# Layer norm in the loaded tile, and a residual that a DMA adds in DRAM

## The chip, the cores and the metric

The kernel runs on one NeuronCore of a Trainium2 chip. The metric is the device time of one execution in microseconds (us), the median of several runs; lower is better. The engines are called PE (matmul), DVE (vector), ACT (scalar), POOL (GpSimd) and SP (which here only issues DMAs). Each works through its own queue strictly in order.

## The reference, cut to what matters

The input is an image of shape (2, 256, 64, 64), seen as two sequences of 4096 positions with 256 channels. Three stages follow: a state-space scan over a group-normed input (layer 0), a bidirectional scan block, and a mixture of eight small feed-forward experts. The change lies in the middle block:

```python
def _core(x, ln_gamma, ln_beta, fp, bp):
    mu = x.mean(-1, keepdims=True)
    var = x.var(-1, keepdims=True)
    xn = (x - mu) / jnp.sqrt(var + 1e-05) * ln_gamma + ln_beta
    y_fwd = _mamba(xn, *fp)
    y_bwd = jnp.flip(_mamba(jnp.flip(xn, 1), *bp), 1)
    return y_fwd + y_bwd + x
```

Here the block's input is itself already a normalised tensor. The kernel therefore takes two roots from one variance: `r1`, which normalises the incoming tensor into the block's `x`, and a second factor that gives `xn` from it in one step. The block's output is the sum of both scans, of `x`, and of the tensor before that normalisation; the running sum is kept in DRAM as `t_dram`.

## The kernel before

**Jobs, chunks, slots.** There are six scan jobs: for each of the two batches a layer-0 job (256 inner channels), a forward job and a backward job (512 inner channels each; the code calls the backward one `flip`). A job runs over 8 chunks of 512 positions. A chunk of 256 inner channels is 16 slots long, one of 512 is 32. In each slot DVE does one scan instruction (L774, 128x1024), so the starts of the 1280 scans tell which slot runs at which time. Numbering the chunks 0 to 47, the forward chunks are 8 to 15 and 32 to 39, the backward ones 16 to 23 and 40 to 47.

**The work of a slot.** POOL forms the scan's input (`bq`, L738) and multiplies some results by C (L799); ACT forms the decays (`da`, L748) in PSUM; DVE scans (L774) and multiplies the other results by C (L783); PE sums over the states (L807).

**The order.** A table (`sl.put(slot, queue, fn)`) places everything else by hand: the next chunk's preparation, the previous chunk's output projection, weight loads. What is put is emitted in slot order, and each engine keeps that order. A planner (`experts`) fills PE and ACT room that is left, by counts of planned work (`sl.count`), with the experts' matmuls of finished columns; what does not fit there is done after the last scan, in a second stage bound to PE.

**The layer norm of a forward chunk** (`norm`, L350 to L445) runs about 45 slots ahead of its chunk. SP loads the columns from `t_dram` into tile `x` (`load_x`, L371); PE takes the mean (L390); DVE writes `cen` = `x` - mean (L396); ACT squares it into tile `nx` (L400); PE takes the variance (L405); ACT takes the two roots; DVE forms the normalised residual in `nx` (L415) and the doubly normalised tensor in `cen` (L416); POOL adds the residual, `x += nx` (L419); ACT then writes gamma and beta applied to `cen` into `nx` (L423), which overwrites what POOL has just read; SP stores `nx` to `n2_dram` for the backward job (L429) and `x` back to `t_dram` (L430). Tile `x` has one buffer and is also used by layer 0; `nx` has two; `cen` has one.

**The output of a chunk** (`finish`, L822 to L857): SP loads the running sum into `xr` (one buffer, L830), PE projects and adds (L837, L839) at slots 16 and 18 of the next chunk (7 and 8 for a 256-channel job), ACT copies into `xr` (L854), SP stores to `t_dram` (L855). The load stands 10 slots before the end of the chunk, and not before slot 21 when the chunk before was a 512-channel one.

**Features** (`features`, L859 to L898), after each backward chunk but the last: mean of `xr`, `fcen` = `xr` - mean by DVE into tile `cen` (L872), squares on ACT, variance, divide by DVE (L887), store to `nf_dram` (L892) for the experts.

**The softplus part of a chunk's preparation** (L582 to L598) holds a tile of three shared buffers named `th` until SP has stored it (`dtd<-sp`, L598).

Of the kernel before, what the change touches and what calls it, by code (L numbers as in the profile page):

```python
# [42 lines left out]
F32 = mybir.dt.float32  # L43
AF = mybir.ActivationFunctionType
ALU = mybir.AluOpType
AX = mybir.AxisListType

P = 128
NB, C, L = 2, 256, 4096
KC = C // P  # L50
T = 512
NCH = L // T
# [19 lines left out]
SLOTS = {  # L72
    2: dict(xs=(-23, -22), conv=(-20,), dbc=-16, dt=(-14, -13), z=(-10, -9), out=(7, 8)),
    4: dict(
        xs=(-31, -30, -24, -23), conv=(-26, -21), dbc=-17, dt=(-15, -13, -11, -9), z=(-6, -5, -3, -2),
        out=(16, 18),
    ),
}
AHEAD = 3
# [55 lines left out]
def hybrid_kernel(ctx: ExitStack, tc: tile.TileContext, a: dict, out: bass.AP):  # L135
    nc = tc.nc
# [14 lines left out]
    mean_w = mean_col.to_broadcast([P, P])  # L151
# [17 lines left out]
    t_dram = [drp.tile([P, KC, L], F32, name=f"t_dram{b}") for b in range(NB)]  # L169
# [10 lines left out]
    def rsqrt(dst, src, eps, scale=1.0):  # L180
        nc.scalar.activation(dst, src, AF.Ln, bias=eps, scale=scale)
        nc.scalar.activation(dst, dst, AF.Exp, scale=-0.5)

    def over_channels(t):
        return t.rearrange("p (o t) -> p o t", o=1).to_broadcast([P, KC, T])
# [6 lines left out]
    with ExitStack() as st:  # L192
        wp = st.enter_context(tc.tile_pool(name="wp", bufs=1))
        wk = st.enter_context(tc.tile_pool(name="wk", bufs=1))
# [19 lines left out]
        sl = Slots()  # L214
# [130 lines left out]
        steps = [(job, c) for job in jobs for c in range(NCH)]  # L345
        starts = [sum(8 * job.nj for job, _ in steps[:i]) for i in range(len(steps) + 1)]
# [3 lines left out]
        def norm(i):  # L350

            (job, c), ck, tag, s0 = steps[i], cks[i], tags[i], starts[i]
            s = job.cols(c)
            b = job.batch
            if job is jobs[AHEAD]:
                return

            def alloc():
                ck["nx"] = wk.tile([P, KC, T], F32, tag="nx", name=f"nx_{tag}", bufs=2)

            if job.flip:
                def load():
                    alloc()
                    nc.sync.dma_start(ck["nx"], n2_dram[b][:, NCH - 1 - c, :, :])
                sl.put(s0 - 44, "sp", load)
                return

            def load_x():
                ck["x"] = wk.tile([P, KC, T], F32, tag="x", name=f"x_{tag}")
                src = t_dram[b] if job.layer else a["x"][b].rearrange("(k p) l -> p k l", p=P)  # L370
                nc.sync.dma_start(ck["x"], src[:, :, s])  # L371

            if job.layer == 0:
                def scale():
                    alloc()
                    for k in range(KC):
                        nc.scalar.activation(
                            ck["nx"][:, k, :], ck["x"][:, k, :], AF.Identity,
                            bias=job.gb[:, k : k + 1], scale=job.gs[:, k : k + 1],
                        )  # L380
                sl.put(s0 - 32, "sp", load_x)
                sl.put(s0 - 25, "act", scale)
                return

            def mean():
                ck["ps"] = psp.tile([P, T], F32, tag="ps", name=f"mean_{tag}")
                for k in range(KC):
                    nc.tensor.matmul(  # L390
                        ck["ps"], mean_w, ck["x"][:, k, :], start=(k == 0), stop=(k == KC - 1)
                    )

            def centre():
                ck["cen"] = wk.tile([P, KC, T], F32, tag="cen", name=f"cen_{tag}")
                nc.vector.tensor_tensor(ck["cen"], ck["x"], over_channels(ck["ps"]), ALU.subtract)  # L396

            def square():
                alloc()
                nc.scalar.activation(ck["nx"], ck["cen"], AF.Square)  # L400

            def variance():
                ck["var"] = psp.tile([P, T], F32, tag="ps", name=f"var_{tag}")
                for k in range(KC):
                    nc.tensor.matmul(  # L405
                        ck["var"], mean_w, ck["nx"][:, k, :], start=(k == 0), stop=(k == KC - 1)
                    )

            def roots():
                ck["r1"] = psp.tile([P, T], F32, tag="ps", name=f"r1_{tag}")  # L410
                rsqrt(ck["r1"], ck["var"], eps5)
                rsqrt(ck["var"], ck["var"], eps10, scale=1.0 + 1e-5)

            def divide():
                nc.vector.tensor_tensor(ck["nx"], ck["cen"], over_channels(ck["r1"]), ALU.mult)  # L415
                nc.vector.tensor_tensor(ck["cen"], ck["cen"], over_channels(ck["var"]), ALU.mult)  # L416

            def add():
                nc.gpsimd.tensor_tensor(ck["x"], ck["x"], ck["nx"], ALU.add)  # L419

            def affine():
                for k in range(KC):
                    nc.scalar.activation(  # L423
                        ck["nx"][:, k, :], ck["cen"][:, k, :], AF.Identity,
                        bias=lngb[:, 1, k : k + 1], scale=lngb[:, 0, k : k + 1],
                    )

            def store():
                nc.sync.dma_start(n2_dram[b][:, c, :, :], ck["nx"])  # L429
                nc.sync.dma_start(t_dram[b][:, :, s], ck["x"])  # L430

            late = 1 if NCH < i < 2 * NCH else 0
            for d, queue, fn in (
                (-48, "sp", load_x), (-44, "pe", mean), (-43, "dve", centre), (-42, "act", square),
                (late - 41, "pe", variance), (late - 40, "act", roots), (late - 39, "dve", divide), (late - 39, "pool", add),
                (-35 if c else -38, "act", affine), (-34, "sp", store),
            ):

                sl.put(s0 + d + (6 if c == 0 else 0), queue, fn)
            s0 += 6 if c == 0 else 0  # L440
            sl.count(s0 - 44, 2, 0, (1,))
            sl.count(s0 - 43, 0, 1)
            sl.count(s0 - 41, 2, 4, (2,))
            sl.count(s0 - 40, 0, 0, (1,))
            sl.count(s0 - (36 if c else 39), 0, 2.3)  # L445
# [376 lines left out]
        def finish(i):  # L822
            (job, c), ck, tag = steps[i], cks[i], tags[i]
            s, b = job.cols(c), job.batch
            v = {}

            def load():
                v["x"] = wk.tile([P, KC, T], F32, tag="xr", name=f"xr_{tag}")
                src = t_dram[b] if job.layer else a["x"][b].rearrange("(k p) l -> p k l", p=P)
                nc.sync.dma_start(v["x"], src[:, :, s])  # L830

            def over_time(m):
                return v["x"][:, m, ::-1] if job.flip else v["x"][:, m, :]

            def project(m):
                v[m] = psp.tile([P, T], F32, tag="ps", name=f"o_{tag}_{m}")
                nc.tensor.matmul(v[m], ident, over_time(m), start=True, stop=False)  # L837
                for j in range(job.nj):
                    nc.tensor.matmul(  # L839
                        v[m], job.w["out"][:, j, m * P : (m + 1) * P], ck["sz", j],  # L840
                        start=False, stop=(j == job.nj - 1),
                    )

            s0 = starts[i + 1]

            before = steps[i - 1][0].nj if i else 0
            sl.put(max(s0 - (10 if job.nj == 4 else 5), starts[i] + (21 if before == 4 else 0)), "sp", load)

            slots = SLOTS[job.nj]["out"] if i + 1 < len(steps) else (3, 4)
            for slot in slots:  # L850
                sl.count(s0 + slot, 1 + job.nj, 1, (1,))
            for m, slot in enumerate(slots):
                sl.put(s0 + slot, "pe", lambda m=m: project(m))
                sl.put(s0 + slot + 1, "act", lambda m=m: nc.scalar.copy(over_time(m), v[m]))  # L854
            sl.put(s0 + slot + 2, "sp", lambda: nc.sync.dma_start(t_dram[b][:, :, s], v["x"]))  # L855
            if job.flip and i + 1 < len(steps):
                features(b, NCH - 1 - c, v, s0 + slot + 2)  # L857

        def features(b, c, v, s0):  # L859
# [8 lines left out]
                    )  # L868

            def centre():  # L870
                v["cen"] = wk.tile([P, KC, T], F32, tag="cen", name=f"fcen_{b}{c}")
                nc.vector.tensor_tensor(v["cen"], v["x"], over_channels(v["ps"]), ALU.subtract)  # L872

            def square():
# [217 lines left out]
        for g in range(nq):  # L1092
            i, jp, n = quads[g]
# [47 lines left out]
    with ExitStack() as st:  # L1141
# [5 lines left out]
        n, x, y, acc, wts, wb, lt, w_dram = {}, {}, {}, {}, {}, {}, {}, {}  # L1147
        q = T // P
# [417 lines left out]
```

## Time and profile before

| | |
|---|---|
| median of 3 runs | 5031.76 us (5031.76 to 5034.15) |
| the profiled execution | 5034.19 us, of which the span from first to last instruction is 5032.4 us |
| busy in the span | POOL 4361.3 us, DVE 4569.8, PE 4249.7, ACT 3614.0 |
| scans (chunks 0 to 47) | 62 to 4476 us; the rest is the experts' second stage |
| forward chunks | 530.5 to 1428.2 us and 2729.0 to 3607.9 us |
| backward chunks | 1428.2 to 2299.3 us and 3607.9 to 4476.4 us |

Busy time adds the durations of instructions. A DVE or POOL instruction starts a little before the one ahead of it has ended, so sums of busy time can exceed the stretch they are taken over; how long an engine stood idle is read from its waits.

### The profile page before, as it was taken

How to read it: one execution, taken by the hardware profiler on the slowest of the kernel's cores; microseconds unless marked ns; L12 is line 12 of the kernel's file. 1: busy time of each engine (PE TensorE's matmuls, PEld its weight loads, DVE VectorE, ACT ScalarE, POOL GpSimd, SP SyncE). 2: the span in 40 equal slices, each digit the busy share in tenths (PEclk: the TensorE clock that was granted, in tenths of full speed). 3: DMA queues.
4: the chain of work that ended last, by engine and by line, in shares of the span. 5: the costliest groups of instructions: out<-in, count | busy, mean ns of one | idle time of the engine just before them, and what ended most of it. 6: DMA issues, size and time to landing. Idle time of an engine off the chain costs nothing. (4 is left out here: it accounts for less than half of the span.)

```text
span 5032.4 us, 47312 instructions
## 1 busy us (share of the span) xinstructions
PE 4249.7 (84%) x14912; PEld 1477.5 (29%) x14912; DVE 4569.8 (91%) x3097; ACT 3614.0 (72%) x7303; POOL 4361.3 (87%) x1426
## 2 busy tenths in 40 slices
PE   5777778788777899989999998989868899889998
PEld 1222222222222233333333332323212333234443
DVE  6998999999999999999989999999999999955654
ACT  5777777777777787887787788878767878752222
POOL 5998999999999999999999999999999999950000
PEclk8778889899887999999999999999989999999999
DMA  5445444444454555447675555554434554446643
GB/s 190 154 171 183 158 167 154 154 152 156 153 176 138 180 173 172 160 169 246 243 240 207 174 173 185 169 186 171 158 131 155 181 195 168 170 151 217 208 155 117
DMA packets 334319, 875.26 MB, mean 174 GB/s; under 512 B 36250, under 2 KB 111796, under 8 KB 292084
## 3 DMA queue, kind: packets, MB, share of 16 engines
q1 hardware_dynamic: 329140, 842.73, 48.6%
q0 software_dynamic: 4928, 29.51, 1.7%
q8 instruction: 118, 1.93, 0.2%
q14 instruction: 133, 1.09, 0.1%
HBM read 673.27 MB, written 198.84 MB: 173 GB/s over the span
## 5 line engine op out<-in xcount | busy, mean ns | idle before, releaser
L738 POOL TENSOR_TENSOR bq<-rxdt,bc 128x2048 f32<-128x2048 f32 x640 | 2892.5, 4542 | 17.3 <-DMA rxdt<-xdtd 9.8
L748 ACT ACTIVATE da<-rdt,w_a 128x512 f32<-128x512 f32 x2560 | 1757.3, 686 | 109.9 <-DVE bq L774 63.4
L774 DVE TENSOR_TENSOR_SCAN da<-da,h_state,bq 128x1024 f32<-128x1024 f32 x664 | 1559.0, 2348 | 55.0 <-ACT da L748 44.9
L799 POOL TENSOR_TENSOR bq<-bq,bc 128x2048 f32<-128x2048 f32 (+1 forms) x280 | 1180.0, 4214 | 22.5
L774 DVE TENSOR_TENSOR_SCAN bq<-da,h_state,bq 128x1024 f32<-128x1024 f32 x456 | 1059.9, 2340 | 23.4 <-ACT da L748 23.4
L807 PE MATMUL y<-bq,stack 128*32 128x512 f32 x5120 | 747.8, 670 | 267.5 <-POOL bq L799 244.0
L783 DVE TENSOR_TENSOR bq<-da,bc 128x1024 f32<-128x1024 f32 x760 | 927.1, 1220 | 15.7
L988 PE MATMUL e<-eh,ew 128*128 128x512 f32 x1376 | 670.2, 621 | 64.8 <-DVE sp L587 12.6
L793 ACT COPY h_state<-da 128x2 f32<-128x2 f32 x759 | 119.1, 157 | 619.6 <-DVE bq L783 617.8
L759 ACT ACTIVATE bq<-h_state,bq,a 128x1 f32<-128x1 f32 x1120 | 429.9, 384 | 2.8 <-POOL bq L738 2.2
L988 PEld LDWEIGHTS e<-eh,ew 128*128 128x128 f32 x1376 | 250.4, 194 | 475.6 <-issue 234.9
L451 PE MATMUL z<-nx,w_in 128*128 128x512 f32 x640 | 329.4, 644 | 62.3 <-DVE nx L415 21.0
L807 PEld LDWEIGHTS y<-bq,stack 128*32 128x32 f32 x5120 | 140.9, 116 | 812.4 <-POOL bq L799 350.1
L524 PE MATMUL conv<-xs,w_conv 64*64 64x512 f32 x2560 | 330.3, 602 | 22.5 <-ACT xs L508 20.3
L1317 ACT ACTIVATE h<-hp,of,sc 128x512 f32<-128x512 f32 x168 | 130.5, 777 | 302.8 <-PE hp L1313 288.7
L988 PE MATMUL e<-en,ew 128*128 128x512 f32 x688 | 323.3, 603 | 24.8 <-DVE fcen L887 17.2
L451 PE MATMUL xs<-nx,w_in 128*128 128x512 f32 x640 | 317.6, 625 | 21.3 <-DVE xc L537 8.5
L839 PE MATMUL o<-sz,w_out 128*128 128x512 f32 x640 | 296.0, 602 | 0.0
L1001 ACT ACTIVATE eh<-e,of,sc 128x512 f32<-128x512 f32 x344 | 259.1, 767 | 44.3 <-PE e L988 44.1
L591 POOL TENSOR_TENSOR xdt<-sp,xc 128x512 f32<-128x512 f32 x160 | 203.3, 1275 | 46.1 <-DVE sp L587 46.1
L774 DVE TENSOR_TENSOR_SCAN da<-da,bq 128x1024 f32<-128x1024 f32 x96 | 219.5, 2286 | 4.4 <-ACT da L748 2.4
L814 PE MATMUL y<-xc,w_d 128*128 128x512 f32 x320 | 186.6, 667 | 20.0 <-DVE sz L820 19.8
(144 smaller groups left out, 4722.0 us busy)
## 6 DMA issues: line engine op xcount, KB each, us to landing
rxdt<-xdtd SPq DMA_DIRECT2D x160, 1024.0 KB, 6.8
rdt<-dtd SPq DMA_DIRECT2D x160, 1024.0 KB, 6.5
bc<-bcd SPq DMA_DIRECT2D x384, 256.0 KB, 3.2
ew<-in_W SPq DMA_DIRECT2D x172, 256.0 KB, 5.0
u<-u SPq DMA_DIRECT2D x86, 512.0 KB, 5.8
u<-eu SPq DMA_DIRECT2D x82, 512.0 KB, 4.3
dtd<-sp SPq DMA_DIRECT2D x160, 256.0 KB, 3.5
xdtd<-xdt SPq DMA_DIRECT2D x160, 256.0 KB, 3.4
```

The costliest lines, as they stand in the source:

```text
L451: nc.tensor.matmul(ps, job.matrices["in", half][:, k, j * P : (j + 1) * P], rhs, start=(k == 0), stop=(k == KC - 1),)
L524: nc.tensor.matmul(v[r][64 * col : 64 * col + 64, :], job.matrices["conv"][rows, 2 * jp + j, k, :], ck["xs", jp][rows, j, k : k + T] if k ...
L738: nc.gpsimd.tensor_tensor(bq[g], ck["rxdt", j], over_groups(ck["bc", 0, sg]), ALU.mult)
L748: nc.scalar.activation(da[g, h][:, k, :], cks[i]["rdt", j][:, q, :], AF.Exp, scale=steps[i][0].w["a"][:, j, q * SG + sg : q * SG + sg + 1],)
L759: nc.scalar.activation(bq[g][:, q, 0:1], job.h[:, j, sg, q : q + 1], AF.Identity, scale=cks[i]["a0", j][:, h, sg : sg + 1], bias=bq[g][:, ...
L774: nc.vector.tensor_tensor_scan(b if on_pool(g, h) else d, d, b, job.h[:, j, sg, 2 * h : 2 * h + 1] if c else 0.0, ALU.mult, ALU.add,)
L783: nc.vector.tensor_tensor(bq[g][:, two, :], d, cks[i]["bc", 1, sg].rearrange("p (o t) -> p o t", o=1).to_broadcast([P, 2, T]), ALU.mult,)
L799: nc.gpsimd.tensor_tensor(b, b, cks[i]["bc", 1, sg].rearrange("p (o t) -> p o t", o=1).to_broadcast([P, groups, T]), ALU.mult,)
L807: nc.tensor.matmul(y[i, j][q * CG : (q + 1) * CG, :], stack, bq[g][:, q, :], start=False, stop=(sg == SG - 1),)
L839: nc.tensor.matmul(v[m], job.w["out"][:, j, m * P : (m + 1) * P], ck["sz", j], start=False, stop=(j == job.nj - 1),)
L988: nc.tensor.matmul(ps, ew[l][:, k, m * P : (m + 1) * P], key[x][:, k, :], start=(k == 0), stop=(k == KC - 1),)
L1001: nc.scalar.activation(key[dst][:, m, :], key["ps", l, m], AF.Relu, bias=of[:, l, e, m : m + 1], scale=sc[:, l, e, m : m + 1],)
```

## The change

It changes where the layer norm of a forward chunk is worked, who adds its residual, and where the features are worked.

- `load_x` of a forward chunk takes one of the two `nx` buffers at the load, at slot -48 instead of at the squares at -42, and the columns are loaded into it. Mean, centre, second division and affine all work in that tile.
- The squares go to a tile `q` of the tag `x`, which later takes the normalised residual.
- POOL's add is replaced by a DMA that POOL issues, which adds `q` to `t_dram` in DRAM. The store of `x` by SP is gone.
- The features' centre works in `xr` itself, so `xr` is held until the store to `nf_dram`.
- The load of `xr` in a backward chunk moves from 10 slots before its end to 2 slots before it.
- The last backward chunk of the first batch (chunk 23) projects at slots 7 and 8 of the next chunk instead of 16 and 18, and its features follow from there.

```diff
 def load_x():
-    ck["x"] = wk.tile([P, KC, T], F32, tag="x", name=f"x_{tag}")
+    if job.layer:
+        alloc()
+        ck["x"] = ck["nx"]
+    else:
+        ck["x"] = wk.tile([P, KC, T], F32, tag="x", name=f"x_{tag}")
...
 def centre():
-    ck["cen"] = wk.tile([P, KC, T], F32, tag="cen", name=f"cen_{tag}")
-    nc.vector.tensor_tensor(ck["cen"], ck["x"], over_channels(ck["ps"]), ALU.subtract)
+    nc.vector.tensor_tensor(ck["x"], ck["x"], over_channels(ck["ps"]), ALU.subtract)

 def square():
-    alloc()
-    nc.scalar.activation(ck["nx"], ck["cen"], AF.Square)
+    ck["q"] = wk.tile([P, KC, T], F32, tag="x", name=f"q_{tag}")
+    nc.scalar.activation(ck["q"], ck["x"], AF.Square)
...
 def divide():
-    nc.vector.tensor_tensor(ck["nx"], ck["cen"], over_channels(ck["r1"]), ALU.mult)
-    nc.vector.tensor_tensor(ck["cen"], ck["cen"], over_channels(ck["var"]), ALU.mult)
+    nc.vector.tensor_tensor(ck["q"], ck["x"], over_channels(ck["r1"]), ALU.mult)
+    nc.vector.tensor_tensor(ck["x"], ck["x"], over_channels(ck["var"]), ALU.mult)

 def add():
-    nc.gpsimd.tensor_tensor(ck["x"], ck["x"], ck["nx"], ALU.add)
+    nc.gpsimd.dma_start(t_dram[b][:, :, s], ck["q"], accum_op=ALU.add)
...
 def store():
     nc.sync.dma_start(n2_dram[b][:, c, :, :], ck["nx"])
-    nc.sync.dma_start(t_dram[b][:, :, s], ck["x"])
...
-    sl.put(max(s0 - (10 if job.nj == 4 else 5), starts[i] + (21 if before == 4 else 0)), "sp", load)
-    slots = SLOTS[job.nj]["out"] if i + 1 < len(steps) else (3, 4)
+    sl.put(max(s0 - (2 if job.flip else 10 if job.nj == 4 else 5), starts[i] + (21 if before == 4 else 0)), "sp", load)
+    slots = SLOTS[2 if i == AHEAD * NCH - 1 else job.nj]["out"] if i + 1 < len(steps) else (3, 4)
...
 # features
-    v["cen"] = wk.tile([P, KC, T], F32, tag="cen", name=f"fcen_{b}{c}")
+    v["cen"] = v["x"]
     nc.vector.tensor_tensor(v["cen"], v["x"], over_channels(v["ps"]), ALU.subtract)
```

## The prediction

> **What bounds the kernel now.** I first cut the span by stages. The slices of the page show POOL and DVE at 9 in almost every slice up to about 4476 us, and the starts of the scans give the chunks. The windows view over one forward chunk of each batch and one backward chunk then reads (columns: stretch, its length, then busy us and instructions of PE, PEld, DVE, ACT and POOL, the granted clock, DMA):
>
> ```profile
> 862.90:975.60 112.70, 89.17 (x358) 28.26 (x357) 111.18 (x78) 88.17 (x184) 112.14 (x39) 0.89 0.46 160
> 3057.60:3167.50 109.90, 99.22 (x365) 34.59 (x364) 108.06 (x71) 90.45 (x185) 109.34 (x36) 0.97 0.52 174
> 4042.10:4150.90 108.80, 99.62 (x365) 34.13 (x364) 106.67 (x70) 88.04 (x182) 107.66 (x35) 0.97 0.53 179
> ```
>
> POOL is busy for 112.1 of 112.7 us, 109.3 of 109.9 and 107.7 of 108.8. The 2.8 us between the two forward chunks are about the two extra POOL products (1.27 us each) that batch 0 carries for the work done ahead for batch 1. So POOL sets the pace of a forward chunk. DVE is close behind. The waits view of DVE over the first of these chunks has one wait worth the name (us, times, longest):
>
> ```profile
> DVE da L774 <- ACT da L748: 0.9, 1, 0.9
> ```
>
> The same view of POOL there has no line at all. Over the six forward chunks in which norms run (8 to 13, 530.5 to 1313.5 us with chunk 14) POOL waits 0.6 us. Who is held by the add itself is in the view of L419:
>
> ```profile
> L419 POOL TENSOR_TENSOR x<-x,nx x16: 2337/2349/2380, 402.7 to 3371.8; 128x1024 f32<-128x1024 f32 x16
> ...
> who waited for it (us, times):
>   ACT nx L423: 5.3, 6
>   DVE da L774: 0.4, 1
> ```
>
> ACT's affine waits for the add, because it overwrites what the add reads. In chunk 11 ACT stands 0.88 us before L423 at 966.39 us, the next decay is late, and that is DVE's 0.9 us.
>
> Backward chunks have another picture. SP's waits, DVE's waits over 3607.9 to 4368.5 us, what ACT's L582 waits for, and a piece of SP's timeline:
>
> ```profile
> SPq L830 <- DVE fcen L872: 35.9, 15, 4.8
> ```
> ```profile
> DVE sp L587 <- ACT h_state L793: 6.3, 6, 1.5
> ```
> ```profile
>   DMA dtd<-sp: 24.4, 10
> ```
> ```profile
> 4110.66 0.57 SPq L598 DMA_DIRECT2D xdtd<-xdt  x1
> 4113.65 0.55 SPq L830 DMA_DIRECT2D xr<-t_dram  x1
> 4114.29 0.55 SPq L598 DMA_DIRECT2D dtd<-sp  x1
> ```
>
> SP stops at the load of `xr`, whose buffer is freed by the features' centre; the store of the softplus tile queues behind it, together with 512 KB of load. The chain that ended last runs through exactly this store (4.81 us from 4114.29 us). ACT then lacks a `th` buffer, and DVE stands 1.0 to 1.6 us per chunk at L587.
>
> **What the Trainium skill says.** "GPSIMD Engine Reference", section 3.1, gives 4497 ns for a two-input add of 2048 floats on POOL; here L738 takes 4542 and the half-sized L419 2349, so the page agrees. "DMA: Bandwidth & Descriptors", section "SWDGE vs HWDGE vs iDMA", says that an accumulating DMA has to be issued by GpSimd, whose cores write its descriptors; so POOL still pays something for each. "SBUF — State Buffer", section "Who interferes with whom", says that a DVE instruction with at most one SBUF input does not contend with GpSimd. The scan and L783 read one operand from PSUM; DVE's L783 takes 1220 ns beside a POOL that never rests, which fits.
>
> **The change part by part.**
>
> *A. POOL in forward chunks.* Removed: 16 adds of 2.35 us, 37.6 us. Added: 16 DMA issues. The trace has no accumulating issue into DRAM. The nearest rows are the 13 issues of L1202, some of which accumulate, and the one plain issue on the strided `t_dram`:
>
> ```profile
> L1202 POOL DMA_DIRECT2D nm<-nf_dram x13: 528/556/897, 4538.1 to 4832.6; - x13
> ```
> ```profile
> L1169 POOL DMA_DIRECT2D n<-t_dram x1: 717/717/717, 4831.9 to 4831.9; - x1
> ```
>
> The plain ones take 0.53, the accumulating 0.89, the strided layout adds 0.19; and the one issue that follows an arithmetic instruction directly (4466.62 us) took 0.73 where its like took 0.53. I take 0.89 + 0.19 = 1.1 us; the bounds are 0.7 and, with the last 0.2 doubled, 1.5. That is 17.6 us, so POOL has 20 us less to do (14 to 26), 1.25 us per norm.
> How much of it comes out depends on DVE. Without its waits DVE needs about 111.7 of the 112.7 us in batch 0 (it waits 0.9 + 0.2), and in batch 1 about 108.3 of 109.9 (the like chunk 2947 to 3058 has 1.1 + 0.4 + 0.2). Its main wait there is the one behind the add, which goes too. So I take 1.0 us per chunk in batch 0 and 1.1 in batch 1, six chunks each: 12.6 us. The other four norms (of chunks 8, 9, 32, 33) run in layer-0 chunks where DVE waits mostly for ACT and PE (1.7 at the mean and 2.0 at the roots for chunk 8): 0.6 each, 2.4 us. Bounds for A: 6 (DVE gives only half) and 20 (POOL alone).
>
> *B. SP in forward chunks.* One 512 KB store (0.54 us of issue) less per norm. SP is not on the path there: nothing gained. Loading into `nx` six slots earlier waits for the buffer of two chunks before, whose last reader is at slot -66 against -48: nothing. At the first norm, layer 0 and the norm share the two buffers; the last layer-0 scale then waits for the gate matmul of the chunk before, over at 365.9 us, and ACT gets there at 369.1. The load itself no longer waits for that scale (SP stood until 370.67 us), worth 0 to 3 us in a chunk of 61 us; I take 1.
>
> *C. Backward chunks.* The load of `xr` leaves slot 22, so SP's 35.9 us there go, and the store of the softplus tile lands about 2 us earlier. DVE's waits at L587, 6.3 us in each batch, would vanish. But POOL is nearly full here too: its own waits over chunks 16 to 22 and 40 to 46 are 3.8 and 2.5 us, 6.3 in all, and no more can come out. I take 4 (0 to 6.3). At its new place, slot 30, the load needs the `nf_dram` store landed: issued near slot 28, 3.9 us to landing, so SP may stop for up to 2 us, with stores of that moment behind it that nobody waits for within two slots. The projection is 18 slots away. For the very last chunk the load falls at about 4466 us and PE needs it at 4483.99: covered; without that cover it would cost its 5 us.
>
> *D. Centre in place.* DVE now has to wait until the store of `xr` (L855) has been read out. Landing takes 3.1 us in the median; the centre starts 4.4 to 4.6 us after the issue in most chunks, and the least slack seen is 0.4 us. Behind it on DVE stand the scans. I take 1 us in all, bounds 0 and 6.
>
> *E. Chunk 23's projection at 7 and 8.* Its last gate is at slot 2, so PE has what it needs. Its work moves 9 to 10 slots earlier in the planner's counts. Worked through by the planner's rule, the experts placed stay 86, with shifts of a few slots between 640 and 805 only; the second stage keeps its 42. I take 0 (-3 to 3).
>
> Sum: -12.6 - 2.4 - 1 - 4 + 1 = -19. I keep 17, since DVE, ACT and POOL are all within 2% of full and small delays of one show in the others. The profiled execution took 5034.2, 2.4 above the median; taken from the median, 5031.8 - 17 = **5015 us**.
>
> **Rivals.**
> *1. POOL alone binds.* Then A gives all 20, C its 6 and B 3: about 5031.8 - 29 = 5003. For it: POOL has no wait. Against: DVE has 1.1 us of slack per chunk.
> *2. DVE is the wall already.* The 0.9 us behind the add turns up at another ACT wait, A gives 4, C 1, D takes 1: about 5028. For it: L587's wait lies where POOL is full.
> *3. Slower: descriptor writing is held up by DVE.* "SBUF — State Buffer" has a case of an issue of 620 ns that took 3100 beside a DVE copy. If the 1.1 us became 1.1 + 2.5 = 3.6, POOL would have 16 x 1.25 = 20 us more; less C that is 5048. It decides from 2.35 us per issue on. Against: no DVE copy stands in those chunks, and the issue at 4466.62 us, with DVE scanning, took 0.73.
> That the sum doesn't stay off POOL is rival 3; that the DMA orders after some other transfer of `t_dram` is no better founded, since the store L430 waits for no such transfer now.
>
> **How the numbers follow.** A measurement can tell 0.2%, 10 us. Main case 0.53, rival 1 0.16, rival 2 0.17, rival 3 0.14. Faster by more than 10 us: nearly all of the first two, 0.68; within: rival 2 and a remnant, 0.18; slower 0.14. The range goes from 4999, under rival 1, to 5036, over rival 2 with D at its bound; it leaves out rival 3 and the far end of rival 1.
>
> **What would show it.** Right: L419 a DMA issue of about 1.1 us; forward chunks of 111.7 and 108.9 us instead of 112.7 and 110; no wait of ACT's L423 on POOL; in backward chunks no wait of DVE at L587 and SP's wait on the centre gone; waits of DVE at the centre under 0.3 us each. Wrong: an issue over 2 us, POOL waits before it, or forward chunks unchanged with DVE free of waits (rival 2).

## The result, and the profile after

| | before | after |
|---|---|---|
| median | 5031.76 us (20 runs) | 5024.28 us (20 runs) |
| ratio, 95% interval | | 0.9984 (0.9978 to 0.9990) |
| span of the profiled execution | 5032.4 us | 5019.1 us |
| POOL busy | 4361.3 us | 4342.0 us |

The change saves 7.5 us; the interval of the ratio allows 5 to 11. The forecast was 5015, a gain of 17. The sign was right and the time lies in the range, but the gain is under half the forecast, less than the 10 us that the prediction called tellable, and nearer to rival 2 (5028). The two profiled executions differ by 13.3 us, of which 5.8 lie in the second stage; runs of other kernels below spread from 549.6 to 557.2 us in that stage, so nothing is read from it.

I cut both traces at the starts of the scans, as in the prediction. Each number of the next table is the difference of two such starts, in us (chunk 47 ends with its last scan), from one trace of each kernel; the last columns are experiments told below.

| chunks | before | after | forward alone | backward alone | load alone | chunk 23 as before | xs earlier |
|---|---|---|---|---|---|---|---|
| 9-13, forward, batch 0 | 563.8 | 567.3 | 567.2 | 564.1 | 563.8 | 567.2 | 563.4 |
| 16-22, backward, batch 0 | 761.4 | 755.2 | 760.5 | 756.1 | 755.3 | 755.4 | 755.4 |
| 23, the turn | 109.7 | 112.1 | 110.2 | 112.6 | 112.1 | 112.0 | 110.8 |
| 24-31, layer 0, batch 1 | 429.7 | 430.9 | 427.6 | 434.4 | 430.0 | 429.8 | 430.4 |
| 32-39, forward, batch 1 | 878.9 | 872.6 | 872.1 | 877.5 | 879.0 | 872.3 | 872.0 |
| 40-46, backward, batch 1 | 760.6 | 755.7 | 760.3 | 754.4 | 755.3 | 755.1 | 755.4 |
| 47, the last | 108.0 | 110.4 | 109.3 | 110.3 | 109.4 | 109.5 | 111.3 |

The gain is in the backward chunks and in batch 1's forward chunks. Batch 0's forward chunks, from which I expected most, became slower.

**POOL got what was promised.** The windows view of the kernel after, over a forward chunk of each batch, with the columns of the prediction:

```profile
863.60:976.80 113.20, 90.18 (x358) 27.53 (x357) 111.29 (x78) 88.19 (x184) 110.89 (x38) 0.91 0.47 159
3052.60:3162.40 109.80, 98.27 (x366) 34.11 (x364) 108.13 (x71) 90.53 (x186) 108.15 (x36) 0.97 0.55 176
```

The fifth busy column, POOL, fell from 112.14 to 110.89 in the first row, the 1.25 us per norm of the prediction. Yet the chunk takes 113.2 us instead of 112.7. The issue in the view of L422:

```profile
L422 POOL DMA_DIRECT2D t_dram<-q x16: 1049/1068/1288, 403.4 to 3368.0; - x16
...
DMA to landing us min/median/max: 5.8/6.9/9.6
```

**Batch 0's forward chunks: one wait went, another grew.** Waits of ACT over chunks 9 to 13, of the kernel before and after (us in all, times, longest):

```profile
ACT da L748 <- DVE bq L774: 12.6, 20, 1.6
...
ACT nx L423 <- POOL x L419: 3.7, 5, 0.9
ACT thx L533 <- PE conv L524: 1.8, 5, 0.4
```
```profile
ACT thx L535 <- PE conv L526: 9.5, 5, 3.2
```

The wait for POOL's add is gone, as planned. But DVE's 0.9 us per chunk did not hang on it. The waits of DVE over these chunks, before and after:

```profile
DVE da L774 <- ACT da L748: 4.8, 6, 0.9
DVE xc L537 <- ACT thx L533: 1.0, 5, 0.2
```
```profile
DVE da L776 <- ACT da L750: 4.5, 5, 0.9
DVE xc L539 <- ACT thx L535: 4.5, 9, 1.8
```

The first line of each is the same wait, 0.9 us once per chunk at slot 25, with and without the add: the decay is late there because ACT itself stood 1.6 us for DVE's scan one slot before. It can't come from the add, since in chunk 11 of the kernel before DVE's wait ends 18 us ahead of ACT's:

```profile
948.14 2.36 DVE L774 TENSOR_TENSOR_SCAN da<-da,h_state,bq 128x1024 f32<-128x1024 f32 x1 [0.90 <-ACT da L748]
```
```profile
966.39 0.81 ACT L423 ACTIVATE nx<-cen,lngb 128x512 f32<-128x512 f32 x1 [0.88 <-POOL x L419]
```

The second line has grown: DVE now waits 4.5 us for the tanh of the convolution instead of 1.0, and the difference of 3.5 us is about what the five chunks lost (563.8 to 567.3).

**Why the convolution is late.** Waits of PE over the same chunks, before and after:

```profile
PE y L807 <- POOL bq L799: 47.5, 19, 5.4
```
```profile
PE y L809 <- POOL bq L801: 27.6, 11, 5.4
...
PE conv L526 <- ACT xs L510: 10.3, 5, 2.5
```

POOL runs further ahead, so PE gets its sums earlier, ends them earlier, and reaches the convolution before ACT has copied its input (tile `xs`). PE's timeline in chunk 12, before and after (start, length, instructions, idle before):

```profile
1011.19 3.90 PE L524 MATMUL conv<-xs,w_conv 64*64 64x512 f32 x29
```
```profile
1009.49 1.07 PE L526 MATMUL conv<-xs,w_conv 64*64 64x512 f32 x2
1013.07 6.11 PE L526 MATMUL conv<-xs,w_conv 64*64 64x512 f32 x27 [2.51 <-ACT xs L510]
```

After an idle of 2.51 us, 27 matmuls take 6.11 us where 29 took 3.90: 1.05 us each instead of 0.59 (medians). Counted from the chunk's start the convolution begins 2.9 us earlier than before (32.7 against 35.6 us), stops, goes on at 36.3 and ends 2.9 us later (43.7 against 40.8).

The trace also records the clock that PE was granted. In it every stretch at half clock, but one at the trace's edge, lasts a whole number of windows of 3.41 us, and all these windows lie on one grid. Two of them in chunk 12 (PE's busy time stands first after the length, the clock third from the end):

```profile
1008.67:1012.08 3.41, 1.89 (x5) 0.19 (x3) 3.38 (x3) 1.60 (x5) 3.41 (x2) 1.00 0.00 0
1012.08:1015.49 3.41, 2.42 (x12) 0.79 (x16) 3.41 (x3) 3.32 (x7) 3.41 (x1) 0.50 0.01 2
```

The clock fell to half after a window in which PE had been busy for 1.89 us, while PE still stood, and stayed there for two windows, to 1018.91. In chunks 10, 11 and 13 it was half for one window; in chunk 9, where PE stood only 1.24 us, not at all. By the profile's busy times, over this whole trace no window at full clock with less than 1.46 us of busy PE was followed by another one at full clock, and none with more than 2.54 us by one at half; in between both occur. The Trainium skill, "TensorE: Matmul & The Clock Gate", Part 1, says that PE's clock is half after an idle window of about 3.4 us and full again after about as much sustained work, the window running freely. The length of the window and its free running agree with the trace; that the window has to be idle does not. A stop shorter than a window is enough, if it leaves little work in one.

### The profile page after: what moved, and what is told of

The parts are those of the page before. It is cut to its first block, busy times and chain, and to the rows that moved or that the text cites. A ratio compares the mean times of both kernels' runs of the same rounds, so it can differ in the third digit from the quotient of the medians.

```text
span 5019.1 us, 47338 instructions
## 1 busy us (share of the span) xinstructions
PE 4247.8 (85%) x14912; PEld 1470.6 (29%) x14912; DVE 4570.5 (91%) x3097; ACT 3616.0 (72%) x7303; POOL 4342.0 (87%) x1426
## 5 line engine op out<-in xcount | busy, mean ns | idle before, releaser
L740 POOL TENSOR_TENSOR bq<-rxdt,bc 128x2048 f32<-128x2048 f32 x640 | 2893.1, 4542 | 17.4 <-DMA rxdt<-xdtd 8.0
L801 POOL TENSOR_TENSOR bq<-bq,bc 128x2048 f32<-128x2048 f32 (+1 forms) x280 | 1180.1, 4215 | 22.6
L761 ACT ACTIVATE bq<-h_state,bq,a 128x1 f32<-128x1 f32 x1120 | 429.8, 384 | 3.4 <-POOL bq L740 2.7
L526 PE MATMUL conv<-xs,w_conv 64*64 64x512 f32 x2560 | 349.1, 621 | 32.9 <-ACT xs L510 30.7
L990 PE MATMUL e<-en,ew 128*128 128x512 f32 x688 | 328.0, 610 | 25.5 <-DVE xr L889 17.4
```

The lines of the kernel that those rows point to most:

```text
L526: nc.tensor.matmul(v[r][64 * col : 64 * col + 64, :], job.matrices["conv"][rows, 2 * jp + j, k, :], ck["xs", jp][rows, j, k : k + T] if k ...
L740: nc.gpsimd.tensor_tensor(bq[g], ck["rxdt", j], over_groups(ck["bc", 0, sg]), ALU.mult)
L761: nc.scalar.activation(bq[g][:, q, 0:1], job.h[:, j, sg, q : q + 1], AF.Identity, scale=cks[i]["a0", j][:, h, sg : sg + 1], bias=bq[g][:, ...
L801: nc.gpsimd.tensor_tensor(b, b, cks[i]["bc", 1, sg].rearrange("p (o t) -> p o t", o=1).to_broadcast([P, groups, T]), ALU.mult,)
L990: nc.tensor.matmul(ps, ew[l][:, k, m * P : (m + 1) * P], key[x][:, k, :], start=(k == 0), stop=(k == KC - 1),)
```

## The experiments

My theory after the result, in three parts: (1) the backward gain comes from one edit, the later load of `xr`; (2) batch 0's forward chunks are held by DVE (with ACT), so POOL's relief brings nothing there and costs the late convolution; (3) chunk 23's slots give some back. The main rival: POOL's relief is the gain, the backward edits are idle.

**1. The forward half alone.** All edits of `norm` and `load_x`; `cen`, the load and chunk 23 as before.

> Only the forward half of the change: layer norm worked in the loaded tile, its residual added by the DMA that POOL issues; features keep a centred tile of their own, xr is loaded at slot -10, chunk 23's projection stays at slots 16 and 18. My theory (the gain sits in the backward chunks; in batch 0's forward chunks DVE and ACT are already the wall, and what POOL gives back there is spent in a late convolution): forward chunks 9 to 13 take 112.7 to 114.5 us as in the changed kernel and not 111.7, DVE waits again at xc for thx (3 to 6 us over these chunks), backward chunks stay at 108.8 with the 6.3 us of waits at sp; in all -3 us against the kernel before (-7 to +3). Rival (POOL's relief is the gain, the backward part gives nothing): -7 to -9 us, and forward chunks of batch 1 account for it.

Measured: 5029.0 us, ratio 0.9993 (0.9986 to 0.9999), that is -3.5 us (-0.5 to -7). Chunks 9 to 13 take 567.2 (the changed kernel 567.3), with the same 4.5 us of waits at `xc`; chunks 32 to 39 gain 6.8; the backward chunks stay. In them DVE still stands for the softplus tile, waits of DVE over chunks 40 to 46:

```profile
DVE sp L589 <- ACT h_state L795: 6.4, 6, 1.3
```

So the forward half gives some 3.5 of the 7.5 us: 6.8 gained in batch 1, 3.4 lost in batch 0.

**2. The backward half alone.**

```diff
-sl.put(max(s0 - (10 if job.nj == 4 else 5), ...), "sp", load)
-slots = SLOTS[job.nj]["out"] if i + 1 < len(steps) else (3, 4)
+sl.put(max(s0 - (2 if job.flip else 10 if job.nj == 4 else 5), ...), "sp", load)
+slots = SLOTS[2 if i == AHEAD * NCH - 1 else job.nj]["out"] if i + 1 < len(steps) else (3, 4)
-    v["cen"] = wk.tile([P, KC, T], F32, tag="cen", name=f"fcen_{b}{c}")
+    v["cen"] = v["x"]
```

> Only the backward half: features centred in xr, xr loaded at slot -2 before a backward chunk, chunk 23's projection at slots 7 and 8; the forward norm with its POOL add as before. My theory: backward chunks 18 to 22 and 42 to 46 at 107.4 to 107.9 us instead of about 109, no wait of DVE at sp, SP's wait for the centre gone; forward chunks 9 to 13 at 112.7 with no wait at xc. From that -11 us of backward chunks, up to 4 us given back at chunks 23 to 31: -7 to -11 us against the kernel before. Rival (POOL's relief is the gain): 0 to -3 us.

Measured: 5024.53 us, ratio 0.9987 (0.9980 to 0.9993), -6.5 us (-3.5 to -10). Backward chunks -5.3 and -6.2; 2.9 lost in chunk 23, 4.7 in 24 to 31. The rival is out. The centre in place, step D, shows in the waits of DVE over chunks 16 to 22 as one line:

```profile
DVE xr L872 <- DMA t_dram<-xr: 0.3, 1, 0.3
```

**3. The later load of `xr` alone.** Only the first line of the diff above.

> One edit alone: the load of xr for a backward chunk moved from slot -10 to -2; the features keep a centred tile of their own, all else is as before. My theory says that this edit frees SP and brings the store of the softplus tile forward, so the waits at sp (6.3 us in each batch) go and backward chunks come to 107.4 to 107.9: -9 to -11 us against the kernel before, as much as the whole backward half or a little more, since chunk 23 is left alone. Rival (the own centred tile, which the load had to wait for, has to go as well for SP to be free, or chunk 23's new slots are part of the gain): under half of it, -4 us or less.

Measured: 5021.8 us, ratio 0.9979 (0.9970 to 0.9987), -10.6 us (-6.5 to -15). One edit does as much as the whole change (5 to 11 us); the intervals overlap. The waits of DVE over chunks 16 to 22, all of them:

```profile
DVE da L774 <- ACT da L748: 1.7, 5, 0.4
DVE bq L774 <- ACT da L748: 1.5, 1, 1.5
```

The wait at L587 (6.3 us before) is gone with the features still in `cen`, so giving up that tile was not needed. Chunk 23 is 2.4 us longer here too, although its slots are untouched.

**4. Chunk 23's projection back at slots 16 and 18.**

```diff
-slots = SLOTS[2 if i == AHEAD * NCH - 1 else job.nj]["out"] if i + 1 < len(steps) else (3, 4)
+slots = SLOTS[job.nj]["out"] if i + 1 < len(steps) else (3, 4)
+    if (b, c) == (0, 0):
+        v["cen"] = wk.tile([P, KC, T], F32, tag="cen", name=f"fcen_{b}{c}")
```

> The changed kernel with chunk 23's projection back at slots 16 and 18 (the very first features in a centred tile of their own, all others in xr). My theory: chunks 23 and 24, 2.4 and 2.1 us longer in the changed kernel, and the shifts of the experts up to chunk 31 come from the new slots: chunks 23 to 31 fall from 543.0 to about 539.5 us, so -3 to -4 us against the changed kernel, about -11 against the kernel before. Rival (the 3.6 us come from POOL and the loads around the turn, not from the slots): within 1 us of the changed kernel, -7 to -8 against the kernel before.

Measured: 5022.92 us, ratio 0.9978 (0.9969 to 0.9988). Against the changed kernel that is 1.4 us by the medians and 3 by the ratios, and the intervals overlap. Chunks 23 to 31 take 541.8, not the 539.5 of my theory: chunk 24 is back at 48.8 (50.9 with the new slots), but chunk 23 stays at 112.0. My attribution of chunk 23 to its slots was wrong. What the new slots cost can't be told: chunks 24 to 31 take 427.6 to 433.8 us in the traces with the old slots and 430.4 to 434.4 in those with the new, and two kernels with the same instructions there differ by 4 us (experiments 5 and 6, 434.3 and 430.4).

**What makes chunks 23 and 47 longer: POOL's lead, by way of PE and ACT.** Each product of L738 feeds two scans. I measured, from the trace, the time from its end to the start of the first of them, and took the least in each chunk. In chunks 42 to 46 of the kernel before it grows: 4.6, 6.3, 7.1, 7.4, 7.6 us. In the kernel after it shrinks from chunk 43 on: 5.9, 5.4, 4.9, 4.4, and it is 4.4 in chunk 47 as well. Four chunks need 64 products. In chunks 43 to 46 POOL begins 64 before and 63 after: with DVE faster, it lives on its lead.

The scans themselves still get their products in time. What comes late is POOL's other work, the products with C that PE sums (L799 before, L801 after). In chunk 47 PE waits for one of them until 25.5 us into the chunk before and 28.2 us after. First that sum before, then the same sum after, with ACT's decay for slot 12 and its scan:

```profile
4393.96 3.46 PE L807 MATMUL y<-bq,stack 128*32 128x512 f32 x16 [3.12 <-POOL bq L799]
```
```profile
4386.71 2.56 PE L809 MATMUL y<-bq,stack 128*32 128x512 f32 x16 [3.08 <-POOL bq L801]
...
4394.91 1.40 ACT L750 ACTIVATE da<-rdt,w_a 128x512 f32<-128x512 f32 x2
...
4396.40 2.36 DVE L776 TENSOR_TENSOR_SCAN da<-da,h_state,bq 128x1024 f32<-128x1024 f32 x1 [1.14 <-POOL bq L740]
```

The last line puts the wait down to POOL's L740, but that scan's product had ended 5.2 us earlier; what ended last was the decay, at 4396.31. ACT had stood 1.2 us for experts' matmuls just ahead of it, and PE had begun these 1.9 us later in the chunk than before. Before, DVE has no wait at slot 12. This is 1.1 of the 2.4 us that chunk 47 is longer. At slot 29 DVE waits for a decay too, 2.9 us instead of 1.7, which is the rest. In chunk 23 the two are 1.9 and 0.5 us. The wait at slot 12 is there in experiment 3 and not in experiment 1, so it comes with the load; the one at slot 29 is as long in experiment 1 (3.1 us in chunk 47), and why it varies stays open. The chain through PE and ACT is read from the traces; no experiment tests it.

**5. PE kept busy ahead of the convolution.** On the changed kernel:

```diff
+if jp == 1 and NCH < i <= 2 * NCH + 1:
+    for _ in range(3):
+        nc.tensor.matmul(v[0], ident, ck["nx"][:, 0, :], start=True, stop=True)
 for k in range(5):
```

> The changed kernel with three more matmuls (ident times nx, into the tile that the convolution then overwrites) ahead of the second convolution of chunks 9 to 17; they do nothing but fill the 2.2 to 2.5 us in which PE stood before it. My theory (PE at half clock after that idle makes the convolution late, then thx, then DVE's xc): the convolution's matmuls take 0.59 us again and not 1.05, DVE's waits at xc over chunks 9 to 13 fall from 4.5 to about 1 us, these chunks from 567.3 to 564 us, so -3 to -4 us against the changed kernel. It stays at 112.6 per chunk then, not at 111.7, since DVE's work is the wall. Rival (the order of ACT's work makes thx late, PE's clock is a bystander): the waits stay at 4 to 5 us, or grow by the 1.3 us that the three matmuls take.

Measured: chunks 10 to 13 take 112.7 us each. The convolution of chunk 12 in the changed kernel, and with PE kept busy (least, median, longest in ns), then the waits of DVE over chunks 9 to 13:

```profile
L526 PE MATMUL conv<-xs,w_conv x96: 587/590/1109, 981.6 to 1019.0; 64*64 64x512 f32 x96
```
```profile
L529 PE MATMUL conv<-xs,w_conv x96: 587/589/640, 982.5 to 1017.8; 64*64 64x512 f32 x96
```
```profile
DVE da L779 <- ACT da L753: 4.5, 5, 0.9
DVE xc L542 <- ACT thx L538: 1.9, 6, 0.9
```

Matmuls that compute nothing made the chunks faster, and the recorded clock stays full through the convolutions of chunks 10 to 13; so the clock, not ACT's order, was the cause. Of the 1.9 us left, 0.9 are one wait in chunk 9, which takes 113.7 us here; the five chunks come to 564.4 (567.3 without). The whole run: 5021.48 us, ratio 0.9982 (0.9975 to 0.9988), beside 0.9984 of the changed kernel: 1 us less where I expected 3 to 4, and the intervals overlap, so the gain of 2.8 us in these chunks is not seen in the whole.

**6. Two xs projections one slot earlier.** On the changed kernel, chunks 9 to 17:

```diff
-at = dict(at, xs=(-31, -29, -24, -23), log=-18)
+at = dict(at, xs=(-31, -29, -25, -24), log=-18)
```

> The changed kernel with the last two of the four xs projections and their copies on ACT one slot earlier in chunks 9 to 17 (slots -25 and -24 instead of -24 and -23), so that what the second convolution waits for is there sooner and PE does not stand before it. My theory: no idle of 2 us before the convolution, full clock, waits at xc near 1 us, chunks 9 to 13 at 563 to 564.5 us. Rival (ACT's order is what matters): ACT's copies one slot earlier push the decay behind them, DVE waits for da instead and the chunks stay at 567 or grow.

Measured: 5017.98 us, ratio 0.9974 (0.9963 to 0.9984), -13 us against the kernel before and, by the ratios, 5 under the changed one, with intervals that overlap. Chunks 9 to 13 take 563.4, and the clock stays full through their convolutions. DVE's waits there are those of the kernel before but for 0.3 us (the wait at `xc` is back at 1.0), while POOL, which then had none, waits for DVE:

```profile
DVE xc L539 <- ACT thx L535: 1.0, 5, 0.2
```
```profile
POOL h_state L800 <- DVE bq L776: 3.9, 4, 1.0
```

With the convolution mended and POOL 1.25 us lighter, the chunk still takes 112.7: not POOL's figure.

**7. Both repairs together** (4 and 6).

> The changed kernel with chunk 23's projection back at slots 16 and 18 and the xs projections of chunks 9 to 17 one slot earlier. If both repairs hold they add up: -1 us (chunk 23's slots, as far as the run of that edit showed) and -3.5 us (forward chunks of batch 0), that is about 5019 to 5020 us and -12 to -13 us against the kernel before. Rival (forward chunks are held by ACT): as the run with chunk 23 as before, -10 to -11.

Measured: 5016.64 us, ratio 0.9974 (0.9963 to 0.9985), the lowest median of kernels that compute everything, and 5 us under the changed kernel by the ratios. It can't be told from experiment 6 alone.

**8. PE kept busy in chunk 37 of the kernel before.** Of batch 1's 6.3 us, 3.5 come from chunk 37 alone (113.0 to 109.5). There the clock worked the other way: in the kernel before, PE stood 3.8 us for POOL and then ran at 1.06 us per matmul, and the experts' matmuls made ACT put off a decay.

```diff
+if (i, j) == (37, 0):
+    for _ in range(6):
+        nc.tensor.matmul(y[i, j], ident, cks[i]["xc", j], start=True, stop=True)
 nc.tensor.matmul(y[i, j], steps[i][0].diagonal[:, j, :], cks[i]["xc", j], start=True, stop=False)
```

> The kernel before with six more matmuls (ident times xc, into the tile that the skip product then overwrites) ahead of the first skip product of chunk 37 and nowhere else. There PE stood 3.77 us for POOL's product, ran at 1.06 us per matmul after it, and DVE stood 3.90 us for a decay that ACT had to put off. My theory (half of what batch 1's forward chunks gained is this one idle, which POOL's relief shortens to 1.2 us): with PE kept busy the matmuls after it take 0.59 us, DVE's 3.90 us fall below 1 and chunk 37 takes about 109.7 us instead of 113.0, although POOL is as late as before. Rival (POOL's lateness itself makes the decay late): the wait stays near 3.9 us and the chunk at 113.

Measured, in the one execution that there is: chunk 37 takes 111.4 us, where I expected 109.7. DVE's longest wait in it, in the kernel before, with PE kept busy, and in experiment 2:

```profile
DVE da L774 <- ACT da L748: 3.9, 1, 3.9
```
```profile
DVE da L774 <- ACT da L748: 2.3, 1, 2.3
```
```profile
DVE da L774 <- ACT da L748: 0.6, 1, 0.6
```

Of the 3.9 us 1.6 went, but the rest isn't all POOL's: the added matmuls hold PE until 1.3 us after POOL's product is done. Experiment 2 tells more. Its forward code is that of the kernel before, POOL's product ends only 0.35 us earlier in the chunk, and PE stands 3.47 us for it; but in its trace the clock stays full after that stop. DVE then waits 0.6 us and the chunk takes 109.8. So most of what chunk 37 loses is the clock, and it isn't lost in every execution. In the kernel after, the product ends 2.7 us earlier in the chunk, PE's wait for it is 1.2 us, and the clock stays full after it.

**9 and 10. DVE relieved, with POOL full and with POOL relieved.** The same line goes from the kernel before (9) and from experiment 6's kernel (10); both then leave out the normalised residual and don't compute the block's result:

```diff
 def divide():
-    nc.vector.tensor_tensor(ck["q"], ck["x"], over_channels(ck["r1"]), ALU.mult)
```

> The kernel before without the first of the two products of each forward norm (normalised value times r1, DVE, 1.21 us, 16 in all); the residual then gets the squares that stand in nx. Only DVE loses work. POOL had no wait at all in chunks 9 to 13 of the kernel before. My theory (before, POOL and DVE are both full in batch 0's forward chunks, so relieving either one alone gives nothing): chunks 10 to 13 stay at 112.5 to 112.7 us, DVE gets waits of about 1.2 us per chunk more, in all 0 to -3 us. Rival (DVE alone is the wall there, POOL follows it): 111.5 us per chunk, -6 us over these chunks and as much in batch 1.

> The changed kernel with two xs projections one slot earlier in chunks 9 to 17 (as in the run of that edit), and without the first product of each forward norm (1.21 us of DVE, 16 in all); the DMA then adds the squares. Here POOL waits about 1.0 us per chunk for DVE (3.9 + 1.0 us over chunks 9 to 13, and a little before). My theory: with DVE relieved as well the chunk shrinks until POOL is full again: 112.7 less 1.0 to 1.2, that is 111.5 to 111.8 us for chunks 10 to 13, and 109.0 to 109.3 instead of 109.7 in batch 1; in all -8 to -12 us against the run with the two projections alone. Rival (ACT's decays and roots set 112.7, not DVE's own work): chunks stay at 112.3 to 112.7 and DVE only waits longer.

Measured: 9 gives 5033.96 us, ratio 1.0008 (1.0001 to 1.0014), slower by some 4 us where I expected 0 to -3; the trace doesn't show why. Chunks 10 to 13 stay at 112.5 to 112.7. 10 gives 5015.45 us, ratio 0.9971 (0.9961 to 0.9980), by the ratios 1.5 us under experiment 6 where I expected 8 to 12, and the intervals overlap; chunks 10 to 13 take 112.0, chunk 35 109.5. Of the waits of DVE over chunks 9 to 13 of 10, the one that experiment 6 does not have:

```profile
DVE da L775 <- POOL bq L800: 2.3, 4, 0.6
```

So 1.21 us less on DVE gives 0.1 where POOL is full and 0.65 where POOL was relieved too; 1.25 us less on POOL alone gave nothing (experiment 6). Both engines hold these chunks.

I had expected 1.0 to 1.2 in 10. The other half is this wait, 0.57 us per chunk at slot 28, and it is not POOL's, although the view says so. In chunk 11 of experiment 9 the same scan has the same wait, and starts before that product of POOL has ended; in 10 the decay ahead of the scan ends at 959.96:

```profile
960.17 2.36 DVE L773 TENSOR_TENSOR_SCAN da<-da,h_state,bq 128x1024 f32<-128x1024 f32 x1 [0.57 <-issue]
```
```profile
958.43 2.34 POOL L798 TENSOR_TENSOR bq<-bq,bc 128x1024 f32<-128x1024 f32 x1
```
```profile
958.56 1.40 ACT L749 ACTIVATE da<-rdt,w_a 128x512 f32<-128x512 f32 x2
```

ACT's decay is what DVE waits for, in 9 and in 10; ahead of it ACT loads a table for 1.28 us. So the rival of experiment 10, ACT, has its part once POOL and DVE are both relieved. No experiment relieves ACT.

## Why the prediction was right or wrong

- **A, the price of the issue: right.** 1.07 us against 1.1 taken; POOL's busy time fell by 19.3 us against 20.
- **A, batch 0: wrong, and the largest miss.** The failing step is "Its main wait there is the one behind the add, which goes too". I saw ACT stand 0.88 us before L423 and DVE lose 0.9 us in the same chunk, and joined them, though DVE's wait ends 18 us before ACT's. The wait is the same without the add (4.5 us in five chunks), so DVE had no 1.0 us to give. Nor does POOL set the pace alone, as the prediction's first part has it. In place of -7.2 us (six chunks and two of 0.6) chunks 8 to 13 show +3.5, the late convolution, and chunks 5 to 7, where the other two norms are worked, show nothing. Rival 2 named this wall; that the change would cost time there no case of mine had.
- **A, batch 1: right in size by luck.** Forecast 6.6 + 1.2 = 7.8, measured 6.3 in chunks 32 to 39. But chunks 33 to 36 gained 0.2 to 0.6 each, not 1.1 (109.7 to 110.1 measured, 108.9 forecast); 3.5 came from chunk 37, mostly by PE's clock, of which the prediction says nothing, and 1.5 from 38.
- **B, 1 us: not to be seen.** Chunks 0 to 7 took 468.5 before, 470.2 after, and 467.7 to 470.6 in the runs of the experiments.
- **C: right mechanism, too small.** SP's wait for the centre and DVE's wait at L587 went, as forecast. The cap "no more can come out" (6.3 us, POOL's own waits) failed: 11.1 us came out of chunks 16 to 22 and 40 to 46, because POOL could draw on its lead as well. Chunks 23 and 47 then paid 2.4 each. The net is 6.3, the upper bound, where I took 4. At its new place the load stops SP for up to 2 us until `nf_dram` is stored, said the prediction; SP's waits for that store over the whole run:

```profile
SPq L832 <- DMA nf_dram<-xr: 2.1, 2, 1.2
```

- **D: 0.3 us in experiment 2 and no wait in the kernel after, inside its bounds,** where I took 1.
- **E: 0 taken, not to be told.** Chunks 24 to 31 are 1.2 us longer in this pair of traces, and kernels with the same instructions there differ by 4.
- **Rivals 1 and 3 are out:** POOL relieved does not set the pace alone (experiments 6 and 10), and the longest issue took 1.29 us. (The 620 and 3100 ns of rival 3 are, in the page's words, times of a whole DMA and not of its issue.)

The measured terms add up to +3.5 (A, batch 0) - 6.3 (A, batch 1) - 6.3 (C net) + 1.2 (E) = -7.9. With chunks 0 to 7 (+1.6) and the time before the first scan (-1.2) the scans end 7.6 us earlier in this pair of traces. The medians differ by 7.5; since one trace of a kernel can be several us off its median, that these agree proves little. The forecast's sign and range held because C gave more than I took and batch 1's gain came by another path; together they outweighed a loss where I had forecast the largest gain.

## What to carry to other kernels

Two waits of like size in one chunk are not a chain until the later one is followed back to its own releaser. An engine that shows no wait may be running ahead rather than holding the pace: measure how far its results lie ahead of their first use, and count the instructions that it begins per period. A view that names the releaser of a wait infers it: where the named instruction ended long before, or ends after, as at slot 12 of chunk 47 and slot 28 of experiment 10, look for what ended last. When an engine that feeds PE gets faster, look where PE's idle time moves to: work reached early and begun after a stop may end later than work reached late without one.

## What the hardware showed unexpectedly

- PE's clock fell to half after windows of 3.41 us in which PE was still busy for up to 2.54 us (kernel after), so a stop of 2.2 to 2.5 us was enough before the convolution; the matmuls then took 1.05 us instead of 0.59 for one or two windows. The length of the last stop alone doesn't tell it: in chunk 37 of the kernel after the clock fell after a stop of 1.5 us, and in chunk 37 of experiment 2 it stayed full after one of 3.47 us.
- Three matmuls that compute nothing, set into that stop, made five chunks 2.8 us shorter (567.3 to 564.4).
- The accumulating DMA into DRAM costs POOL 1.07 us of issue for 512 KB and lands after 5.8 to 9.6 us, median 6.9; nobody waited for it.
